# First attention and first feed-forward: pieces placed by a table of times in rounds, and a written order of steps inside a round

## The chip, the cores and the metric

The kernel runs on one core of a Trainium2 chip. The core has a matrix engine (TensorE, PE in the profile), a vector engine (VectorE, DVE), a scalar engine (ScalarE, ACT), GpSimd (POOL), and SyncE (SP), which issues most transfers. Each takes its instructions in the order in which they stand in its queue, and waits by semaphores for the others. The metric is the time of one execution on the device in microseconds, as the median of several runs. Smaller is better.

## The reference

The network has four pairs of attention and feed-forward over x of 2 × 1024 rows and 256 columns. The change touches the first pair, the start of the second attention, and nothing of what they compute:

```python
x = x + _L0_attn_a_ref(_layernorm(x), Wq, Wk, Wv, Wo)
x = x + _L0_ffn_ref(_layernorm(x), W1, b1, W2, b2, W3, b3)
x = x + _L0_attn_b_ref(_layernorm(x), ...)
...
def _L0_attn_a_ref(X, Wq, Wk, Wv, Wo):       # NH, NKV, HD = 16, 8, 32
    q, k, v = heads(X @ Wq), heads(X @ Wk), heads(X @ Wv)
    q = q * cos + _rotate_half(q) * sin
    k = k * cos + _rotate_half(k) * sin
    k, v = repeat(k, 2), repeat(v, 2)
    att = 50 * tanh((q @ k.T) * 256 ** -0.5 / 50)
    att = softmax(where(causal, att, -inf))
    return (att @ v) @ Wo

def _L0_ffn_ref(x, W1, b1, W2, b2, W3, b3):  # 256, 512, 512, 256
    x = relu(x @ W1.T + b1)
    x = relu(x @ W2.T + b2)
    return x @ W3.T + b3
```

`heads` and `repeat` stand here for reshapes and repeats that are written out in the reference.

## The kernel before

`attn_a_ffn0` (line 385) computes the first attention and, between its steps, the feed-forward of rows whose attention is done. All of x stays on the chip as 16 tiles of 128 rows. The two sequences are cut into two chunks of 512 query rows each, so there are four chunks (b, c), numbered 0 to 3 here. A chunk's attention is made of **rounds**: one round takes four heads, one pair of them after another (u and r run over 2 × 2), and one block kb of 128 keys. The first chunk of a sequence sees 4 key blocks, the second 8, so the four chunks have 16, 32, 16 and 32 rounds, 96 in all. Blocks on the diagonal have 512, 384, 256 and 128 live query columns, the others 512.

The steps of a round (`round_`, line 597):

- *scores* (line 611): four matmuls side by side on PE into two PSUM tiles `s` (two buffers, so a round's scores write the tiles that the tanh of the round before has read), then on ACT a tanh (617) for each half into the tile `pr` (four buffers) and an exponential (622) for each half; on diagonal blocks POOL masks each half (625).
- *weigh* (636): four matmuls that add v times `pr` into the one PSUM bank `py`; then on DVE the sums of probabilities are added to `acc` (646, 650, 653). The first block's `pr` is read only by the sums of the second block. After the last block DVE turns `py` (656).
- *finish* (663): the sums are added over partitions by a matmul (`sm`), DVE turns them (668), takes the reciprocal (670), multiplies (671) and turns back into `yT` (674).

Around the rounds stand **pieces**, each a closure that issues instructions on several engines:

- *norms*: for two row tiles, `stats` (251, 252 on DVE, 254 on POOL) and `rows` (the reciprocal root in nine small DVE instructions, 232 to 242, then 263 on POOL);
- *inputs*, nine for each pair of row tiles: `turn` (four transposes, 278, and the copy `xT`, 281, on DVE), `queries` and `keys` (projections `pq` and `pkv`, 290; the rotary part on DVE, 317 and 326, and POOL, 331), `turn_queries` and `turn_keys` (577 and 585 on PE, 578 and 586 on DVE);
- *outputs*, four for each chunk: the projection with Wo (591) and the addition to x (596);
- the 22 pieces of a feed-forward over 512 rows (`ffn0_pieces`, line 461): six for the norms and turns (484 on PE, the copy 492 on DVE, 476 on POOL for b3), four first hidden blocks, four second hidden blocks in two halves each (502 on PE, the relu 511 on DVE), four outputs (518 on PE, 523 on DVE).

The pieces share three PSUM banks (tag `g`). Inside `in_order` the scheduler leaves the order of PE, DVE, ACT and POOL as it is written, so the program text decides the order on every engine. Before the change a planner spreads the pieces: each has a cost (0.35 to 1.75), every round a weight (its columns + 100), `share` gives each round pieces until its share of cost is spent, and `mixed` merges two lists evenly. A round then issues, in this order: scores of round n (with tanh, exponentials and masks), one piece, weigh of round n − 2 (with the sums, and the turn of `py` after the last block), finish of round n − 3 if it was a last block, and the other pieces. The inputs of chunk 0 and the norms of chunk 1 are issued before round 0. Nine pieces of the third feed-forward (`held`) are kept back and merged with the outputs of chunk 3 after the last round. The feed-forward of chunk 3 is done at the start of `attn_b` (line 729), evenly merged (`interleave(owed, chunks[0].inputs)`) with the first inputs of the second attention.

Of the kernel before, what the change touches and what calls it, by code (L numbers as in the profile page):

```python
# [10 lines left out]
F32 = mybir.dt.float32  # L11
I32 = mybir.dt.int32
BF16 = mybir.dt.bfloat16
AF = mybir.ActivationFunctionType
ALU = mybir.AluOpType
# [24 lines left out]
def interleave_into(out, a, b):  # L40
# [56 lines left out]
SECOND = {  # L97
    "norms": (-30, -20.1, -11.8, -12, -6.4, -2.4),
    "unpack": (-7.9, 2.57, (6.7, 7.6, 10.3, 13.8)),
}  # L100


class Net:
# [281 lines left out]
    def attn_a_ffn0(self, w, wo, cos, sin, ffn):  # L385

        nc, tc = self.nc, self.tc
        with ExitStack() as ctx:
            big = ctx.enter_context(tc.tile_pool(name="a_big", bufs=1))
            work = ctx.enter_context(tc.tile_pool(name="a_work", bufs=2))
            ps = ctx.enter_context(tc.tile_pool(name="a_ps", bufs=1, space=PSUM))
            ones = big.tile([P, 32], F32, name="ones")
            nc.gpsimd.memset(ones, 1.0)
            ctx.enter_context(self.in_order())
            pools = (ps, big, work, w, wo, cos, sin, ones)
            chunks = []  # L400
            for b in range(B):


                kT, v = {}, {}
                chunks += [self.attn_a_chunk(pools, b, c, kT, v) for c in range(2)]

            def bank(name):
                return ps.tile([P, 512], F32, tag="g", name=name, bufs=3)


            after = [self.ffn0_pieces(work, bank, 4 * n, *ffn) for n in range(3)]
            for _, step in chunks[0].norms + chunks[0].inputs + chunks[1].norms:
                step()

            def mixed(a, b):
                out = []
                interleave_into(out, a, b)
                return out

            held = 9  # L420
            rounds, fill = [], []
            for chunk, first, second, third in (
                (chunks[0], chunks[1].inputs + chunks[2].norms, [], []),
                (
                    chunks[1], chunks[2].inputs + chunks[3].norms,
                    chunks[0].outputs + after[0], [],
                ),
                (chunks[2], chunks[3].inputs, chunks[1].outputs + after[1][:6], []),
                (chunks[3], after[1][6:], chunks[2].outputs + after[2][:6], after[2][6:-held]),
            ):  # L430

                weights = [r.columns + 100 for r in chunk.rounds]
                quota = sum(weights[:3]) / sum(weights) * sum(
                    cost for cost, _ in first + second + third
                )
                n = 0
                while n < len(first) and quota > 0:
                    quota -= first[n][0]
                    n += 1
                fill += self.share(weights[:3], first[:n])  # L440
                fill += self.share(weights[3:], mixed(first[n:], second) + third)
                rounds += chunk.rounds
            for n in range(len(rounds) + 3):
                here, turned, ended = (
                    rounds[n - j] if 0 <= n - j < len(rounds) else None for j in (0, 2, 3)
                )
                pieces = fill[n] if n < len(fill) else []
                if here:
                    here.scores()
                for piece in pieces[:1]:  # L450
                    piece()
                if turned:
                    turned.weigh()
                if ended and ended.last:
                    ended.finish()
                for piece in pieces[1:]:
                    piece()
            for _, step in mixed(after[2][-held:], chunks[3].outputs):
                step()

    def ffn0_pieces(self, work, bank, i, w1, w2, w3, b1, b2, b3, scalar=False):
# [77 lines left out]
    def attn_a_chunk(self, pools, b, c, kT, v):  # L539
# [58 lines left out]
        def round_(u, r, kb):  # L598
# [5 lines left out]
            def scores():  # L604
                pr = own.pr = work.tile([P, 4, 512], F32, tag="pr", name="pr", bufs=4)
                tiles = [
                    ps.tile([P, 2, 512], F32, tag="s", name="s", bufs=2) for _ in range(2)
                ]
                for s in range(4):
                    rows = slice(32 * s, 32 * s + 32)  # L610
                    nc.tensor.matmul(  # L611
                        tiles[s // 2][:, s % 2, 0:m], kT[kb // 4][rows, u, kb % 4 * P : (kb % 4 + 1) * P],
                        shared["qT"][rows, u, r, off:512], start=True, stop=True,
                    )
                halves = [pr[:, 2 * h : 2 * h + 2, off:512] for h in range(2)]
                for h in range(2):
                    nc.scalar.activation(  # L617
                        halves[h], tiles[h][:, :, 0:m], AF.Tanh, scale=1.0 / (16.0 * 50.0)
                    )
                for h in range(2):  # L620

                    nc.scalar.activation(halves[h], halves[h], AF.Exp, scale=50.0)  # L622
                    if kb >= 4 * c:
                        d = halves[h][:, :, 0:P]
                        nc.gpsimd.affine_select(  # L625
                            out=d, in_=d, compare_op=ALU.is_ge, fill=0.0, base=0,
                            pattern=[[0, 2], [1, P]], channel_multiplier=-1,
                        )

            def weigh():  # L630
                if kb == 0:
# [3 lines left out]
                for s in range(4):  # L635
# [2 lines left out]
                        pr[:, s, off:512], start=(kb == 0), stop=(kb == end),  # L638
                    )

                if kb == 1:
                    acc = shared["acc"] = work.tile(
                        [P, 4, 512], F32, tag="acc", name="acc", bufs=1
# [7 lines left out]
                elif kb > 1:  # L651
                    acc = shared["acc"][:, :, off:512]
                    nc.vector.tensor_tensor(acc, acc, pr[:, :, off:512], ALU.add)
                if kb == end:
                    own.turned = work.tile([P, 16, 32], F32, tag="tny", name="turned", bufs=1)
                    nc.vector.transpose(own.turned.rearrange("p n d -> p (n d)"), py)

            def finish():

# [2 lines left out]
                for s in range(4):  # L662
                    nc.tensor.matmul(
                        sm[32 * s : 32 * s + 32, :], ones, shared["acc"][:, s, :],
                        start=True, stop=True,
                    )
                sums = work.tile([P, 16, 32], F32, tag="tns", name="turned", bufs=1)
                nc.vector.transpose(sums.rearrange("p n d -> p (n d)"), sm)
                rec = work.tile([P, 16], F32, tag="rec", name="rec")
                nc.vector.reciprocal(rec, sums[:, :, 0])  # L670
                nc.vector.tensor_tensor(
# [3 lines left out]
                    shared["yT"][:, 2 * u + r, :], own.turned.rearrange("p n d -> p (n d)")  # L675
                )

            own.scores, own.weigh, own.finish = scores, weigh, finish
            return own

        chunk = type("chunk", (), {})()
# [47 lines left out]
    def attn_b(self, w, wo, cos, sin, ffn):  # L729
# [9 lines left out]
        with ExitStack() as ctx:  # L739
# [25 lines left out]
                return ps.tile([P, 512], F32, tag="sc", name=name, bufs=7)  # L765

            owed = [step for _, step in self.ffn0_pieces(work, bank, 12, *ffn)]
            interleave(owed, chunks[0].inputs)
            quads, rounds, turns, fill = [], [], {}, {}

            def add(n, step):
# [1387 lines left out]
```

## Time and profile before

| | |
|---|---|
| median of 3 runs | 2913.81 us (2906.41, 2915.19, 2913.81) |
| the profiled execution | 2906.75 us |
| its span, first to last instruction | 2905.0 us |
| mean granted TensorE clock | 0.927 |
| busy over the span: PE, weight loads, DVE, ACT, POOL | 87%, 54%, 69%, 46%, 35% |
| first scores (line 611), round 0 | 46.2 us |
| first scores of rounds 16, 48, 64 | 109.9, 238.8, 306.6 us |
| last addition of the stage (line 523) | 453.3 us |
| first scores of the second attention (line 861) | 508.5 us |

The stage that the change touches thus takes about a sixth of the span, from 0 to 508.5 us. A line of the timeline gives the start, the duration, the engine, the line of the kernel, the operation, the output and its inputs, the shapes, how many such instructions are merged, and in brackets how long the engine had been idle and whose result ended the wait. Matmuls overlap and their ends are modelled, so the distance from one start to the next says more than the duration. A matmul on f32 runs as two passes, and appears as two records.

### The profile page before, as it was taken

Reading aid. Unit: us, or ns where it says so; the run is one execution under the profiler, and the core shown is the slowest. Engines: PE = TensorE matmul, PEld = TensorE weight load, DVE = VectorE, ACT = ScalarE, POOL = GpSimd, SP = SyncE. Lnnn points to the kernel's source line nnn. Section 1 sums busy time; section 2 is a strip of 40 time slices with the busy share of each in tenths; the row PEclk is TensorE's granted clock in tenths of the full one; section 3 lists DMA queues with packets and bytes.
Section 4 is the critical chain, followed back from the end, with each engine's and each line's share of the span. In section 5 each row is a group of like instructions: output and inputs, shape, how many; then the busy total and the mean of one; then the engine's idle time right before and its main releaser. Section 6 shows DMA issues by size and latency. Waiting matters only on the chain.

```text
span 2905.0 us, 66838 instructions
## 1 busy us (share of the span) xinstructions
PE 2530.3 (87%) x26384; PEld 1572.5 (54%) x26384; DVE 2003.4 (69%) x6786; ACT 1329.8 (46%) x2800; POOL 1021.7 (35%) x1568
## 2 busy tenths in 40 slices
PE   6999998999998877988888888888787988898888
PEld 2334334444434444665555555555565776777777
DVE  5777774866758957778777878787657555665551
ACT  2676870345453335666666666757321211221110
POOL 3444242211106757667555655655300000000000
PEclk9999998999999967999999999999887998999999
DMA  3000000000001100000000000000011010110100
GB/s 121 1 1 1 1 1 0 1 1 1 1 1 53 36 1 1 1 1 1 1 1 1 1 1 1 1 1 1 20 31 25 10 25 21 21 31 18 24 9 15
DMA packets 61978, 35.37 MB, mean 12 GB/s; under 512 B 43216, under 2 KB 58080, under 8 KB 61664
## 3 DMA queue, kind: packets, MB, share of 16 engines
q1 hardware_dynamic: 59472, 29.49, 3.9%
q8 instruction: 207, 3.39, 0.5%
q10 hardware_dynamic: 2192, 1.61, 0.2%
q14 instruction: 107, 0.88, 0.1%
HBM read 22.68 MB, written 8.39 MB: 11 GB/s over the span
## 4 chain that ended last, share of the span: by engine, by line
PE 39%; DVE 13%; ACT 4%; POOL 4%; issue 4%; DMA 0%; POOLq 0%; ACTq 0%; DVEq 0%
PE ph L1484 5%; PE po L1993 5%; PE pg L1980 5%; PE pu L1980 4%; DVE p L1247 4%; PE e L1236 4%; PE dT L1308 3%; PE po L1503 2%; DVE p L1286 2%; PE py L1338 1%; POOL p L1294 1%; ACT p L1257 1%; POOL p L1274 1%; PE pq L1663 1%; PE kh L1663 1%
## 5 line engine op out<-in xcount | busy, mean ns | idle before, releaser
L1257 ACT ACTIVATE p<-p,nm 128x128 f32<-128x128 f32 (+7 forms) x512 | 390.8, 767 | 78.7 <-DVE nm L1253 40.9
L1247 DVE CUSTOM_DVE_ANT_0 p<-e,mask 128x512 f32<-128x512 f32 (+3 forms) x768 | 382.1, 551 | 59.5 <-PE e L1236 59.1
L1294 POOL TENSOR_SCALAR p<-p,md 128x128 f32<-128x128 f32 (+7 forms) x256 | 241.0, 945 | 175.5 <-DVE md L1286 147.4
L254 POOL TENSOR_SCALAR ln_mv<-ln_mv 128x2 f32<-128x2 f32 x64 | 15.7, 246 | 722.5 <-DVE ln_mv L252 709.6
L1322 ACT ACTIVATE pT<-dT 128x384 f32<-128x384 f32 (+3 forms) x384 | 176.2, 486 | 202.1 <-PE dT L1308 201.2
L1236 PE MATMUL e<-kT,qT 32*128 32x512 f32 (+3 forms) x1536 | 229.8, 578 | 44.3 <-DVE nm L1247 41.5
L1308 PE MATMUL dT<-ident,p 128*128 128x128 f32 x1152 | 197.0, 297 | 65.8 <-POOL p L1294 35.6
L1286 DVE CUSTOM_DVE_ANT_0 p<-p,nrs 128x128 f32<-128x128 f32 (+7 forms) x256 | 220.3, 885 | 24.7 <-POOL p L1278 24.4
L901 ACT ACTIVATE pr<-s 128x512 f32<-128x512 f32 (+3 forms) x384 | 157.3, 497 | 162.9 <-PE s L896 154.2
L1274 POOL TENSOR_SCALAR p<-p,ra,neg_lam 128x128 f32<-128x128 f32 (+7 forms) x256 | 217.8, 851 | 9.3
L1308 PEld LDWEIGHTS dT<-ident,p 128*128 128x128 f32 x1152 | 137.6, 149 | 153.1 <-POOL p L1294 67.7
L617 ACT ACTIVATE pr<-s 128x1024 f32<-128x1024 f32 (+1 forms) x192 | 145.3, 813 | 131.0 <-PE s L611 83.5
L1993 PE MATMUL po<-down,inter 128*128 128x256 f32 x576 | 160.1, 441 | 1.9 <-DVE x L2000 1.2
L861 PE MATMUL s<-kT,qT 32*128 32x512 f32 (+3 forms) x768 | 155.3, 519 | 3.8 <-DVE q_pad L869 1.9
L1980 PE MATMUL pg<-xT,gate 128*128 128x256 f32 x576 | 151.1, 409 | 5.5 <-ACT xT L283 5.5
L622 ACT ACTIVATE pr<-pr 128x1024 f32<-128x1024 f32 (+1 forms) x192 | 152.1, 852 | 0.0
L869 DVE CUSTOM_DVE_ANT_0 masked<-s,mask 128x128 f32<-128x128 f32 (+3 forms) x256 | 110.6, 487 | 58.9 <-PE s L861 58.8
L1236 PEld LDWEIGHTS e<-kT,qT 32*128 32x128 f32 x1536 | 84.8, 202 | 116.4 <-DVE nm L1247 74.3
L625 POOL TENSOR_SCALAR_AFFINE_SELECT pr<-pr 128x256 f32<-128x256 f32 x128 | 90.1, 722 | 154.7 <-ACT pr L622 57.7
L1986 DVE TENSOR_TENSOR inter<-inter,pu 128x512 f32<-128x512 f32 x72 | 49.3, 684 | 132.7 <-PE pu L1980 132.7
L1993 PEld LDWEIGHTS po<-down,inter 128*128 128x128 f32 x576 | 126.4, 224 | 25.0 <-DVE x L2000 2.0
L1980 PE MATMUL pu<-xT,up 128*128 128x256 f32 x576 | 139.3, 386 | 0.0
(295 smaller groups left out, 5377.2 us busy)
## 6 DMA issues: line engine op xcount, KB each, us to landing
uk_d<-uk SPq DMA_DIRECT2D x128, 32.0 KB, 1.9
r<-uk_d SPq DMA_DIRECT2D x8, 512.0 KB, 3.6
x<-in_L_attn_a_X SPq DMA_DIRECT2D x4, 512.0 KB, 6.9
qh_d<-qh SPq DMA_DIRECT2D x8, 256.0 KB, 2.6
o<-qh_d SPq DMA_DIRECT2D x128, 16.0 KB, 1.7
out<-x SPq DMA_DIRECT2D x4, 512.0 KB, 3.1
w<-in_L_ffn_W2T SPq DMA_DIRECT2D x1, 1024.0 KB, 7.5
pk<-in_L_ffn_gate_packed SPq DMA_DIRECT2D x8, 128.0 KB, 2.5
```

The source lines that it names most:

```text
L861: nc.tensor.matmul(tiles[g][:, 0:n], shared["qT"][rows, t, j * P : (j + 1) * P], kT[rows, lo : lo + n], start=True, stop=True,)
L901: nc.scalar.activation(pr[:, g, off:512], tiles[g][:, 0:m], AF.Exp, scale=0.25)
L1236: nc.tensor.matmul(own.tiles[h][:, a, 0 : hi - lo], made["q"][r : r + 32, a, t, :], kT[r : r + 32, a, lo:hi], start=True, stop=True,)
L1247: nc.vector.tensor_tensor_reduce(own.p[h][a][:, lo:hi], own.tiles[h][:, a, 0 : hi - lo], neg_row[:, T - nk + lo : T - nk + hi], -1.0, 3e38 ...
L1257: nc.scalar.activation(own.p[h][a], own.p[h][a], AF.Exp, bias=own.nm[:, h, a : a + 1], scale=-1.0, accum_out=own.sm[:, h, a : a + 1],)
L1274: nc.gpsimd.tensor_scalar(p1, p1, own.ra[:, h : h + 1], nlam[:, head : head + 1], ALU.mult, ALU.mult)
L1286: nc.vector.tensor_tensor_reduce(p0, p0, p1, own.nrs[:, h : h + 1], 3e38, ALU.add, ALU.min, own.md[:, h : h + 1],)
L1294: nc.gpsimd.tensor_scalar(p0, p0, -1.0, own.md[:, h : h + 1], ALU.mult, ALU.add)
L1308: nc.tensor.transpose(dT[:, n, :], own.p[h][0][:, kb * P : (kb + 1) * P], self.ident)
L1322: nc.scalar.activation(shared[t, s + h][:, lo:hi, :], own.dT[h, part][:, 0 : hi - lo, :], AF.Exp)
L1980: nc.tensor.matmul(ph[:, j, :], m_[:, kc, m * P : (m + 1) * P], f.xT[:, kc, :], start=(kc == 0), stop=(kc == 1),)
L1993: nc.tensor.matmul(f.po[:, b], inter[m // 2][:, m % 2, b * P : (b + 1) * P], wd[:, m % 2, (m // 2) * C : (m // 2 + 1) * C], start=(m == 0) ...
```

## The change

A table `FIRST` gives each piece a time, counted in rounds: negative before round 0, 42.12 for shortly after the start of round 42. All pieces of the stage are put in one list and sorted by it. The steps of a round are split into smaller ones (`scores`, `tanh` and `exp` for each half, `weigh`, `sums`, `turn`, `finish`, `divide`), and the string `round` writes their order: scores, sums, tanh 0, tanh 1, exp 1, exp 0, finish, divide, weigh, turn. `lags` says how many rounds later a step is done. A piece is issued ahead of the step at whose tenth of the round its time falls. Pieces whose times lie behind the last round are issued afterwards. The hand-over to the second attention gets two lists of times of its own.

```diff
+FIRST = {
+    "lags": {"W": 2, "Z": 2, "V": 2, "F": 3, "G": 3},
+    "round": "S Z A0 A1 B1 B0 F G W V",
+    "inputs": (
...
+        (
+            12.2, 13.35, 14.1, 15.15, 16.37, 17.33, 18.16, 23.08, 24.51, 24.94, 25.12,
+            26.54, 27.81, 28.92, 29.68, 30.61, 31.63, 32.76, 33.49, 34.5, 35.34, 34.505,
+        ),
...
+    "ffn": (
+        (
+            26, 26.35, 26.005, 28.76, 29.61, 34.99, 35.96, 36.52, 37.92, 38.3, 39.37,
+            40.663, 41.655, 41.968, 41.973, 41.978, 42.12, 42.137, 43.63, 44.17, 45.33,
+            46.22,
+        ),
...
+    "owed": (
+        0, 1, 2, 2.8, 4.09, 5.62, 6.071, 6.77, 8.216, 8.915, 9.869, 10.824, 12.589, 12.601,
+        13.614, 14.709, 16.685, 17.762, 18.073, 19.179, 20.299, 21,
+    ),
+    "next": (
+        -1.5, 1.69, 4.79, 4.795, 7.431, 9.276, 13.151, 16.167, 16.172, 17.387, 17.392,
+        18.948, 19.543, 19.834, 23.309, 23.314, 28.039, 29.57,
+    ),
+}
...
-            held = 9
-            rounds, fill = [], []
-            for chunk, first, second, third in (
...
-                fill += self.share(weights[:3], first[:n])
-                fill += self.share(weights[3:], mixed(first[n:], second) + third)
-                rounds += chunk.rounds
-            for n in range(len(rounds) + 3):
...
-            for _, step in mixed(after[2][-held:], chunks[3].outputs):
-                step()
+            timed = []
+            for n, chunk in enumerate(chunks):
+                timed += zip(FIRST["inputs"][n], [s for _, s in chunk.norms + chunk.inputs])
+                timed += zip(FIRST["outputs"][n], [s for _, s in chunk.outputs])
+                if n < 3:
+                    pieces = self.ffn0_pieces(work, bank, 4 * n, *ffn)
+                    timed += zip(FIRST["ffn"][n], [s for _, s in pieces])
+            timed.sort(key=lambda x: x[0])
+            rounds = [r for chunk in chunks for r in chunk.rounds]
+            tokens = FIRST["round"].split()
...
+            for n in range(len(rounds) + 4):
+                for k, token in enumerate(tokens):
+                    while timed and (timed[0][0] - n) * len(tokens) <= k + 1e-6:
+                        timed.pop(0)[1]()
+                    m = n - FIRST["lags"].get(token[0], 0)
+                    if 0 <= m < len(rounds) and hasattr(rounds[m], names[token[0]]):
+                        getattr(rounds[m], names[token[0]])(*[int(x) for x in token[1:]])
+            for _, step in timed:
+                step()
...
-            interleave(owed, chunks[0].inputs)
+            timed = list(zip(FIRST["owed"], owed)) + list(zip(FIRST["next"], chunks[0].inputs))
+            for _, step in sorted(timed, key=lambda x: x[0]):
+                step()
```

By these times the PE pieces stand like this in some rounds (h is a first hidden block, h2 half of a second one, between two scores in program order): round 23 a query projection and an output; 41 to 42, after the scores of 41, one h2, weigh, three h2, the scores of 42, two h2, sums matmul, weigh; 49 three projections; 69 three outputs; 64, 88, 91 and 94 none. Chunk 0's inputs take the two query projections of a pair of tiles ahead of its key projections. The third feed-forward keeps its last nine pieces, and chunk 3 three of its four outputs, until after the last round, the outputs first.

## The prediction

> **What bounds the kernel now.** I looked first at the busy time by stretches, cut where the four chunks of the first stage begin: rounds 0–15 start at 46.2 us, rounds 16–47 at 109.9, 48–63 at 238.8, 64–95 at 306.6; the last chunk's end runs from 423.7, and the hand-over to the second attention ends at 508.5. After the span come PE, weight loads, DVE, ACT and POOL busy, then the granted clock.
>
> ```profile
> core 0: us, PE busy (x) PEld busy (x) DVE busy (x) ACT busy (x) POOL busy (x), PEclk, DMA share, GB/s
> 46.20:109.90 63.70, 53.77 (x329) 19.52 (x328) 45.23 (x109) 39.96 (x64) 28.53 (x53) 0.89 0.01 1
> 109.90:238.80 128.90, 123.94 (x732) 46.55 (x728) 98.61 (x167) 100.59 (x128) 53.85 (x59) 0.99 0.00 1
> 238.80:306.60 67.80, 60.01 (x397) 25.51 (x393) 51.48 (x105) 40.99 (x67) 36.01 (x59) 0.95 0.00 1
> 306.60:423.70 117.10, 115.78 (x676) 42.81 (x676) 81.94 (x100) 99.11 (x124) 36.30 (x40) 1.00 0.00 1
> 453.70:508.50 54.80, 41.19 (x136) 22.96 (x136) 26.50 (x84) 3.40 (x8) 17.11 (x35) 0.84 0.00 0
> ```
>
> TensorE (PE) is the bound in every row. The long chunks have little left (PE busy 96% and 99%); both short chunks lose on idle time and on the clock. What a loss looks like, in the timeline at round 16:
>
> ```profile
> 109.94 1.14 PE L611 MATMUL s<-qT,kT 32*128 32x512 f32 x8
> 111.02 0.66 PE L278 MATMUL ln_t<-ident,ln_xn 128*128 128x128 f32 x4
> 111.60 0.64 PE L636 MATMUL py<-pr,v 128*32 128x256 f32 x8
> 114.81 1.98 PE L290 MATMUL pq<-wa,xT 128*128 128x512 f32 x4 [2.58 <-DVE xT L281]
> ```
>
> PE turns the normalised rows at 111.02, and wants the copy (xT, line 281) for its next projection. That copy stands on DVE behind another chunk's norm and the row sums, so PE idles 2.58 us.
>
> **Prices of a round.** I take start to next start, since ends are modelled:
>
> ```profile
> 415.23 1.06 PE L636 MATMUL py<-pr,v 128*32 128x512 f32 x8
> 416.23 1.08 PE L611 MATMUL s<-qT,kT 32*128 32x384 f32 x8
> 417.24 1.99 PE L502 MATMUL ph<-h,w 128*128 128x512 f32 x4
> 419.15 1.07 PE L636 MATMUL py<-pr,v 128*32 128x512 f32 x8
> ...
> 155.46 1.94 ACT L617 ACTIVATE pr<-s 128x1024 f32<-128x1024 f32 x2 [1.47 <-PE s L611]
> 157.28 2.00 ACT L622 ACTIVATE pr<-pr 128x1024 f32<-128x1024 f32 x2
> 159.17 1.02 ACT L617 ACTIVATE pr<-s 128x1024 f32<-128x1024 f32 x1
> ```
>
> Weigh 1.00; one piece (projection or hidden half) 1.91; scores of 512 columns 1.07 (109.94 to 111.02). ACT needs 159.17 − 155.46 = 3.71 for a round of 512 columns; the same view gives 2.86, 2.00 and 1.16 for 384, 256 and 128. So a full round has 3.71 − 2.07 = 1.64 us of PE time beside ACT, somewhat less than one piece. For each round I add the PE steps standing between two scores, in program order, and take the larger of that and ACT. Done over 95 rounds of the old order, most rounds agree with the trace within 0.1 us; what is measured above the sum is stalls and slow clock.
>
> | rounds | PE steps before | larger, before | measured | remainder | larger, after |
> |---|---|---|---|---|---|
> | 0–15 | 45.1 | 48.0 | 63.75 | 15.8 | 51.5 |
> | 16–47 | 119.0 | 121.7 | 128.9 | 7.2 | 127.0 |
> | 48–63 | 55.7 | 57.3 | 67.75 | 10.5 | 58.4 |
> | 64–94 | 110.7 | 116.5 | 117.1 | 0.6 | 118.2 |
>
> **The change, part by part.** No instruction of the stage is added or taken; the compiled order shows other places on PE, DVE and POOL, and ACT's two exponentials swapped. DMAs and SP's queue keep their places, so nothing is moved past a transfer.
>
> *The table* lumps pieces. Round 42 gets five hidden halves (three ahead of its scores), while rounds 64, 65, 88 and 91 get no piece for PE between their scores, or none but small ones. Hence the sums after: +3.5, +5.3, +1.1, +1.7, together 11.6 us worse. ACT's backlog over such a row gives back a little: rounds 80 to 82 measure 11.71 where the larger values add to 12.35. I take 0.5 in each long chunk, −1.0.
>
> *The remainders* are what it can win.
> - Rounds 48–63: the largest stall is 2.76 us at 240.5–242.9, xT again. In the new table the turn is in round 48 and its projection in 49, the norm four rounds earlier; key and query turns come a round or more after their ropes. I leave 2.0 of 10.5: −8.5.
> - Rounds 0–15: rounds 0 and 1 lose 7.6 between them (scores wait for ACT and xT). The new order puts scores 1 ahead of the first turn, so ACT has work during the projection; DVE's second norm still comes first. I leave 5.6 there. DVE's own work in rounds 12–15 sums to 14.7 us in the new order and 14.4 in the old, so 2.0 of the rest stays: 7.6 of 15.8, −8.2.
> - Rounds 16–47: the 2.58 us above goes, as its turn is now a round ahead. DVE's sum in rounds 24–31 is 30.4, a microsecond above PE and ACT. I leave 1.5 of 7.2: −5.7.
> - Rounds 64–94: −0.6.
>
> *Sums (Z) ahead of pieces on DVE.* ACT waits 38 us in all for a probability buffer until the sums have read it; Z at the front ends that. This is inside the remainders. Z waits for POOL's masks two rounds old; behind it stand the pieces' evacuations, and PE's three small banks cover a round.
>
> *Ends.* The first chunk's inputs now run q0, q1 ahead of k0, and DVE's xT ahead of the second norm (xT was 1.16 us late): scores 0 come 1.2 earlier after a wait for the last key turn. At the end two hidden halves fill the wait for the masks at 424–429 us, which lengthens S95-to-sums by 0.7 while the rounds above lose 2.6 of PE work, counted there. All four outputs now follow the division directly: the first needs yT, DVE's four steps after the sums (0.72+0.26+0.69+0.71 = 2.4 less 1.2 of its own early matmuls), +1.2, where a hidden half stood before. In the hand-over the second half's norm comes one norm (1.6 us) earlier on DVE; a later turn costs 0.6: −1.0.
>
> *Clock.* Thin rounds may slow PE. Rows:
>
> ```profile
> 239.40:242.80 3.40, 1.19 (x12) 0.42 (x4) 3.29 (x3) 2.39 (x4) 3.40 (x3) 1.00 0.00 0
> 242.80:246.20 3.40, 3.06 (x10) 1.22 (x11) 1.50 (x2) 1.47 (x2) 3.06 (x6) 0.51 0.00 0
> ...
> 147.20:150.60 3.40, 2.72 (x20) 0.89 (x18) 3.33 (x8) 3.40 (x5) 1.06 (x1) 1.00 0.00 0
> 150.60:154.00 3.40, 3.31 (x4) 1.17 (x4) 3.06 (x15) 3.39 (x4) 1.54 (x3) 0.51 0.00 0
> ```
>
> A stretch with sparse matmuls is followed by 3.4 us at 0.51, which costs PE 1.7. Bounds: none (rounds 72 and 73, PE 3.5 and 3.3 of 3.71, stayed at 1.00) or one after each of nine runs of thin rounds, 15. Rounds 25, 64 and 88 have PE for 1.6 to 1.8 of 3.71, nearest to the second pair; for those three I take 3 in all.
>
> The Trainium skill ("TensorE: Matmul & The Clock Gate", HAM oscillation) gives as its rule no PE gap over about 3.4 us. By that rule the thin rounds, idle at most 2.1 us at a stretch (3.71 − 1.64), would cost 0 in place of 3; the rows above, where gaps of 1 to 2.8 us were enough, speak against relying on it.
>
> Sum: +11.6 − 1.0 − 8.5 − 8.2 − 5.7 − 0.6 − 1.2 + 0.7 + 1.2 − 1.0 + 3.0 = −9.7; the bounds of the two large unknowns are remainders wholly gone but for rounds 0–1 (−5.5 more), or kept (+23), and clock 0 to 15 (−3, +12). The profiled execution took 2906.75 us (span 2905.0); −9.7 gives 2897.1. The median of the three runs is 2913.81, 7.1 higher, which gives 2904.1. I predict between them: **2900 us**.
>
> **Rivals.**
> 1. *Stalls all go, and so does the slow clock.* Remainders to 5.6, clock term 0: −18; the hand-over, where PE idles 13.6 of 54.8 us, gives 5 more: about −23, 2887. For: the new distances between producer and consumer. Against: DVE's 14.7 in rounds 12–15 stays. 0.20.
> 2. *No change to tell.* The remainders keep some 20 of their 34, as DVE, not the order on PE, sets them: the lumps' 11.6 meets 14 won, and the ends and clock add 2: 2910 ± 5. For: POOL's masks stretch beside DVE's sums in any order (line 625 takes 0.41 us at best, 0.71 in the mean). Against: in chunk 3 the same sums leave 0.6. 0.20.
> 3. *Slower: the clock.* Each of the nine runs of thin rounds lets the clock fall for two stretches of 3.4 us: 18 × 1.7 = 31 in place of 3, 2928. It decides from about nine stretches on (9 × 1.7 − 3 = 12). For: 147.2 needed only a part-idle stretch. Against: half of the runs fill PE for 60% of ACT's time. 0.12.
> 4. *That the tables don't bite* is excluded: the compiled order moves on three engines.
>
> The forecast itself has 0.48: 2890 to 2908.
>
> **How the numbers follow.** 0.3%, about what a measurement here can tell from no change, is 8.7 us, 2905 to 2922.5 around the median. The forecast puts 0.40 of its 0.48 under 2905, rival 1 all 0.20: faster 0.60. Rival 2 has 0.15 within, 0.05 above; the forecast's other 0.08 falls within: same 0.23. Rival 3's 0.12 and that 0.05: slower 0.17. The range takes in rival 1's middle and most of the lower half of 3: 2878 to 2922.
>
> **What would show it.** Right: scores 16, 48 and 64 begin near 104, 232 and 293 us; the wait for xT at line 281 gone from the short chunks; rounds 41 and 42 with PE full and ACT idle for some 8 us; rounds 64 and 88 paced by ACT. Wrong: DVE sums still among ACT's waits, or a granted clock below 0.95 in rounds 64 to 95. If rounds 48–63 don't fall below 64 us, the main term has failed.

## The result, and the profile after

The changed kernel takes 2887.84 us in the median of five runs (2884.38 to 2897.69), the kernel before 2906.41 us beside it (2901.01 to 2915.19). The ratio is 0.9935, with a 95% interval from 0.9907 to 0.9964. The profiled execution took 2885.65 us, its span is 2883.9 us, the mean granted clock 0.931. Repeated later on one chip with other kernels, it gave 2889.29 us and 0.9925 (0.9908 to 0.9943). So the change is worth some 19 to 22 us, about twice the 9.7 us that the prediction's sum gave.

The busy time by stretches, cut again at the first scores of rounds 0, 16, 48, 64 and 95, with the hand-over last (after the span come PE, weight loads, DVE, ACT and POOL busy, then the granted clock):

```profile
40.80:96.60 55.80, 51.01 (x329) 19.50 (x328) 45.17 (x108) 41.08 (x62) 31.13 (x52) 0.91 0.01 1
96.60:226.80 130.20, 125.95 (x736) 48.11 (x732) 102.56 (x169) 104.32 (x130) 53.38 (x62) 0.97 0.00 1
226.80:285.40 58.60, 56.36 (x388) 23.97 (x385) 47.30 (x94) 42.75 (x66) 31.28 (x53) 1.00 0.00 1
285.40:403.20 117.80, 114.33 (x676) 42.80 (x676) 83.74 (x108) 100.92 (x122) 35.75 (x43) 1.00 0.00 1
434.50:489.20 54.70, 40.86 (x132) 23.19 (x132) 27.99 (x85) 2.41 (x6) 17.41 (x35) 0.84 0.00 0
```

The rows say where. Rounds 48 to 63 fall from 67.8 to 58.6 us and their clock rises from 0.95 to 1.00. Rounds 0 to 15 fall from 63.7 to 55.8 us and begin 5.4 us earlier. The long chunks (second and fourth row) take what they took. From the first scores to those of round 95 PE idles for 14.5 us instead of 23.6 (gaps of more than 0.15 us between its matmul records), and the clock is at half for 17.1 us instead of 23.9, which is worth up to 3.4. These two make 12.5 of the 15.1 us that the kernel wins there.

| part | forecast | measured, profiled executions |
|---|---|---|
| head, to the first scores | −1.2 | −5.4 (46.19 to 40.77; −4.4 in the repeat, 41.84) |
| rounds 0–15 | −4.7 | −7.9 |
| rounds 16–47 | −0.9 | +1.2 (−0.5 in the repeat) |
| rounds 48–63 | −7.4 | −9.1 |
| rounds 64–94 | +0.6 | +0.7 |
| scores of round 95 to the stage's last addition | +1.9 | +1.6 |
| hand-over | −1.0 | −0.4 |
| clock, as a term of its own | +3.0 | none; it is in the rows above |
| rest of the program, unchanged | 0 | −1.8 |
| sum | −9.7 | −21.1 |

What ACT waits for ahead of its tanh (one group before, one after: busy time and mean, then idle time and its releasers):

```profile
L617 ACT ACTIVATE pr<-s 128x1024 f32<-128x1024 f32 (+3 forms) x190 | 144.7, 817 | 129.9 <-PE s L611 82.3 <-DVE acc L646 27.8 <-DVE acc L653 10.1
```
```profile
L652 ACT ACTIVATE pr<-s 128x1024 f32<-128x1024 f32 (+1 forms) x192 | 144.3, 803 | 99.1 <-PE s L644 92.9 <-DVE acc L685 5.9
```

Of the 37.9 us in which DVE's sums held ACT up, 5.9 are left. The largest such place is round 16, in the timeline of the changed kernel:

```profile
97.11 0.71 DVE L717 STREAM_TRANSPOSE yT<-turned 128x512 f32<-128x512 f32 x1
97.74 1.72 DVE L685 TENSOR_TENSOR acc<-pr 128x1536 f32<-128x1536 f32 x1
99.55 1.94 ACT L652 ACTIVATE pr<-s 128x1024 f32<-128x1024 f32 x2 [2.17 <-DVE acc L685]
100.63 2.99 PE L644 MATMUL s<-qT,kT 32*128 32x512 f32 x8 [1.67 <-ACT pr L652]
102.50 0.69 DVE L340 TENSOR_SCALAR xT<-ln_t 128x512 f32<-128x512 f32 x1
```

Here the division of a finished block (its last step is the turn into `yT`) is on DVE ahead of the sums, the sums hold ACT, ACT holds PE's scores, and a norm's root then stands between the sums and the copy xT. The stall of round 16 that the prediction showed has changed its first link and has not gone.

### The profile page after: what moved, and what is told of

Same layout as the page of the kernel before. It is cut to its first block, busy times and chain, and to the rows that moved or that the text cites. A ratio compares the mean times of both kernels' runs of the same rounds, so it can differ in the third digit from the quotient of the medians.

```text
span 2883.9 us, 66846 instructions
## 1 busy us (share of the span) xinstructions
PE 2519.9 (87%) x26384; PEld 1569.8 (54%) x26384; DVE 2005.4 (70%) x6786; ACT 1340.7 (46%) x2800; POOL 1020.5 (35%) x1568
## 4 chain that ended last, share of the span: by engine, by line
PE 39%; DVE 14%; ACT 4%; POOL 4%; issue 3%; DMA 0%; POOLq 0%; DVEq 0%; SPq 0%; ACTq 0%
PE ph L1531 6%; PE po L2040 5%; PE pg L2027 5%; PE pu L2027 4%; DVE p L1294 4%; PE e L1283 4%; PE dT L1355 3%; PE po L1550 2%; DVE p L1333 2%; PE py L1385 1%; POOL p L1341 1%; ACT p L1304 1%; PE pq L1710 1%; POOL p L1321 1%; PE kh L1710 1%
```

## The experiments

All times to a point of the program are of one profiled execution; ratios are medians against the kernel before on the same chip. "Slow clock" is the time before the scores of round 95 in which the granted clock was about half (the clock records; each stretch is a multiple of 3.41 us). The records begin with the first stretch at full clock, at 22.3 us in the changed kernel and 27.8 us before; ahead of it the matmuls of a projection start 0.85 us apart, behind it 0.43, and this slow start isn't in the column.

| kernel | median | ratio, 95% interval | first scores | from there to round 95 | from there to attn_b's first scores | slow clock |
|---|---|---|---|---|---|---|
| before | – | 1 | 46.19 | 377.5 | 84.8 | 27.3 |
| changed | 2887.84 | 0.9935 (0.9907–0.9964) | 40.77 | 362.5 | 86.0 | 17.1 |
| e0 changed again | 2889.29 | 0.9925 (0.9908–0.9943) | 41.84 | 361.2 | 86.0 | 13.7 |
| e1 old head order | 2893.58 | 0.9945 (0.9925–0.9964) | 44.30 | 363.6 | 85.8 | 23.9 |
| e2 xT late | 2909.22 | 0.9993 (0.9978–1.0007) | 41.16 | 379.3 | 86.0 | 37.6 |
| e3 sums late | 2903.30 | 0.9978 (0.9964–0.9993) | 42.70 | 377.0 | 86.2 | 34.1 |
| e4 filled | 2894.67 | 0.9941 (0.9918–0.9963) | 41.82 | 373.2 | 76.6 | 30.7 |
| e5 before, sums first | 2905.90 | 0.9982 (0.9969–0.9995) | 43.89 | 370.9 | 82.5 | 17.1 |
| e6 before, head and xT | 2901.35 | 0.9965 (0.9951–0.9978) | 41.31 | 371.9 | 86.1 | 20.5 |
| e7 before, all three | 2892.36 | 0.9933 (0.9913–0.9952) | 42.65 | 368.5 | 82.3 | 20.5 |
| e8 filled, mended | 2876.58 | 0.9885 (0.9869–0.9901) | 42.03 | 360.5 | 77.2 | 13.7 |
| e9 filled, mended again | 2877.97 | 0.9886 (0.9867–0.9906) | 41.95 | 362.0 | 77.4 | 23.9 |
| e10 bare rounds | 2895.37 | 0.9941 (0.9920–0.9962) | 42.31 | 363.0 | 86.5 | 17.1 |

### e1: the head in its old order

```diff
 "inputs": ( (
-  -48, -46.195, -45.41, -43.685, -44.19, -43.2, -42, -42.995, -42.695, -38.4, ...
+  -48, -47, -46, -44, -45, -43, -42, -41, -40, -39, ...
```

> The changed kernel with one part of its table undone: chunk 0's projections stand in their old order (q and k of the two halves mixed, each followed by its rotated twin), instead of both q first; xT of the first half still stands ahead of the second norm, and everything from round 0 on is as in the changed kernel. Theory (the order of the projections gave most of the 5.4 us by which round 0 came earlier: 46.19 to 40.77 in the two profiled executions): the scores of round 0 start at 45 to 46.5 again, and the end comes 4 to 5.5 us later than the changed kernel's 2883.9, at 2888 to 2889.5. Rival (only the place of xT counts, which the prediction priced at 1.2 us, and the rest was where the slow-clock stretches happened to fall): the scores of round 0 start at 40 to 43 and the end is within 2 us of 2883.9. What tells them apart is the start of the first scores and the granted clock between 20 and 45 us.

The first scores start at 44.30 us, between what theory (45 to 46.5) and rival (40 to 43) named: 3.5 later than the changed kernel's, and attn_b's first scores come 4.5 later. The medians (0.9945 and 0.9935) can't tell the two kernels apart. PE in the head, first before, then e1, then the changed kernel:

```profile
18.35 3.78 PE L290 MATMUL pq<-wa,xT 128*128 128x512 f32 x4 [1.93 <-DVE xT L281]
23.22 3.75 PE L290 MATMUL pkv<-wa,xT 128*128 128x512 f32 x4 [1.08 <-DMA wa<-in_L_attn_a_Wv]
```
```profile
16.82 3.47 PE L318 MATMUL pq<-wa,xT 128*128 128x512 f32 x4 [0.78 <-DVE xT L309]
23.78 3.39 PE L318 MATMUL pkv<-wa,xT 128*128 128x512 f32 x4 [3.48 <-DMA wa<-in_L_attn_a_Wv]
```
```profile
16.77 6.42 PE L349 MATMUL pq<-wa,xT 128*128 128x512 f32 x8 [0.83 <-DVE rsq_n L291]
23.04 0.38 PE L610 MATMUL t_ps<-ident,qr 128*128 128x128 f32 x2
23.66 0.44 PE L610 MATMUL t_ps<-ident,qr 128*128 128x128 f32 x2 [0.24 <-POOL qr L390]
23.93 3.61 PE L349 MATMUL pkv<-wa,xT 128*128 128x512 f32 x8
```

In before and e1 the key projection waits for a transfer, the weights from Wv. With xT early and the old order PE starts its first query projection at 16.82 instead of before's 18.35, and then idles 3.48 us instead of 1.08 at that wait. The new order puts the second query projection, which needs only weights that are there, into the wait: in the changed kernel Wv's transfer is issued at 16.7 us and lands 6.6 us later, and no wait on it is listed.

Of e1's 3.5 us, some 2.0 are the order and 1.4 the clock. From the key projection to the first scores e1 takes 20.52 us, the kernel before 22.97, and e5 (below, which has before's head) 19.08. The differences are about half of the time at half clock: e1 has such a stretch at 23.3 to 26.7 us, at the end of the idle time; before reaches full clock only at 27.8 us and has a slow stretch at 34.6; e5 is at full clock from 23.2 us on. The ten executions with the new order take 23.8 to 24.0 us from the first query projection to the first scores, with no slow stretch in it. e5 takes 24.62 and begins 1.1 us later, for xT. So xT and the order together are worth some 1.7 us, and the rest of what before loses in the head is mainly the clock.

### e2: xT directly ahead of its reader

```diff
 chunk 1, second turn    -6.35   +8.398     (query projection at 8.4)
 chunk 2, both turns     -16.37  +17.328    -28.92  +29.678
 chunk 3, both turns     -48.01  +49.248    -56.55  +57.853
```

> The changed kernel with the five transposing copies (xT) of chunk 1's second half and of chunks 2 and 3 set directly ahead of the first projection that reads them, as the old planner set them, instead of about one round ahead; every other step keeps its time. Theory (the distance between the copy and its reader is what took the stalls out of rounds 0 to 63): each of the five costs a wait of 1 to 2.8 us on PE again, the waits on xT are back in the list, rounds 48 to 63 go from 58.7 to 61 to 64 us and the whole is 5 to 13 us longer than the changed kernel's 2883.9. Rival (the stalls went because the softmax sums now stand first on DVE, so that the copy itself is done sooner): the waits on xT stay under 0.5 us each, and the whole is within 2 us.

The stage takes 17.2 us more (attn_b's first scores 489.21 to 506.43), above the 5 to 13 expected; rounds 48 to 63 take 64.2 us, at the upper edge. PE's waits by releaser, e2 and the changed kernel from 36 to 430 us (total, times, longest):

```profile
PE pq L318 <- DVE xT L309: 10.9, 6, 4.3
PE s L613 <- ACT pr L621: 10.2, 13, 2.2
```
```profile
PE s L644 <- ACT pr L652: 9.3, 11, 1.7
PE pq L349 <- DVE xT L340: 1.6, 2, 1.0
```

The waits on xT grow by 9.3 us, and all of PE's listed waits together by 6.4 (16.7 to 23.1, since others fall away). The slow clock grows by 20.5 us, which at half speed is worth up to 10.2. Together 16.6, against 17.2 measured: the larger part of these stalls' price is the clock behind them. The rival (under 2 us) is out. The old planner had some of the five turns farther ahead than e2 has, so e2 prices the distance; it doesn't undo the change.

### e3: the sums behind the weighing

```diff
-  "Z": "sums", "V": "turn",
+  "Z": "none", "V": "late",
...
+def late():
+    sums()
+    if kb == end:
+        turn()
```

> The changed kernel with the step Z (the softmax sums on DVE, which free the tanh's output buffers for ACT) put back behind the weighing step, with the V step as before the change; the times of all pieces are kept. Theory (that Z stands ahead is what took the 27.8 and 10.1 us of DVE out of ACT's waits ahead of the tanh): 15 to 40 us of ACT's idle time ahead of the tanh end on DVE's sums again, and because ACT paces the rounds without pieces, the attention stage grows by 3 to 6 us. Rival (ACT was waiting for PE's scores all along and the name of the releaser is all that changes): the time is within 1.5 us of the changed kernel's 2883.9 though DVE is back among the releasers.

```profile
L621 ACT ACTIVATE pr<-s 128x1024 f32<-128x1024 f32 (+1 forms) x192 | 144.2, 802 | 114.4 <-PE s L613 83.9 <-DVE acc L654 25.5 <-POOL pr L630 2.7
```

In this group of e3, DVE's sums hold ACT for 25.5 us again, as the theory said, but the stage takes 16.6 us more (505.83) instead of 3 to 6. PE's listed waits grow by 5.6 us (16.7 to 22.3): on ACT's tanh 13.7 (9.3 in the changed kernel), 3.4 on `acc` ahead of the sums' matmul, while others are shorter. The slow clock grows by 17 us, half of which is 8.5. Together 14.1, against 14.7 counted from the first scores (1.9 of the 16.6 were there already). The rival falls.

### e5, e6, e7: the parts alone on the old grid

e5 takes the kernel before and only moves the sums ahead; e6 only takes the new head order and the turns of rounds 16 and 48 one round earlier; e7 has both.

```diff
 if here:
     here.scores()
+if turned:
+    turned.sums()          # e5, e7; taken out of weigh
 for piece in pieces[:1]:
...
+for n in (16, 48):         # e6, e7
+    fill[n - 1].insert(0, fill[n].pop(0))
...
-for _, step in chunks[0].norms + chunks[0].inputs + chunks[1].norms:
+for k in (0, 1, 2, 4, 3, 5, 7, 8, 6, 9, 10, 12, 13, 11, 14, 16, 15, ...):
```

> The kernel before with one part of the change alone: the softmax sums of a round stand directly behind the scores on DVE (ahead of the round's pieces and of the weighing), the planner, its grid of pieces and the head stay as they were. The previous runs gave 16.6 us (to the first scores of attn_b) for putting the sums back, far over the forecast. Theory (the parts add up, each stall on PE bringing a slow-clock stretch behind it): 10 to 16 us shorter than before's 2905.0, ACT's idle time on DVE's sums falls from 37.9 us to under 10, and the slow-clock time before the last scores falls from 27.3 us to about 17. Rival (the order of the sums pays only together with the new times of the pieces, because in the old grid other things are late at the same places): within 4 us of 2905.0 although ACT no longer waits for DVE.

> The kernel before with two other parts alone: the head's pieces in the new order (chunk 0's two q projections one behind the other, xT ahead of the second norm), and the xT of chunks 2 and 3 that the old grid had in the same round as its first reader (rounds 16 and 48) one round earlier. Sums, grid and hand-over stay. Theory: the head gives its 4 to 5.5 us by itself (first scores at 40.7 to 42), and the two moved copies 2 to 5 us more in rounds 16 to 63 (the waits on xT there, up to 2.6 us each, gone, and a slow-clock stretch less): 2895 to 2899. Rival (what the head gains is lost again in round 1, which waits for the next norm): rounds 0 to 15 grow by what the head gave, and the end is within 2 us of 2905.0.

> The kernel before with all three small parts (sums ahead, the head's new order, xT of rounds 16 and 48 a round earlier), but with the old planner's grid of pieces and the old hand-over. It differs from the changed kernel by the grid alone. Theory (the prediction's sum: the new times of the pieces pair them worse with the rounds and cost 11.6 us in lumps, which the stalls' end had to pay for): this kernel is faster than the changed one by 5 to 12 us, at 2872 to 2879. Rival (the grid's spacing is itself what keeps DVE and POOL from being late, and the sum over rounds overstates the lumps): slower than the changed kernel by 2 to 10 us, at 2886 to 2894, with waits on POOL's masks and turned copies left.

e5: attn_b's first scores come at 497.3 instead of 508.5, −11.1, with ACT's waits on the sums at 12.4 us (not quite under 10) and 17.1 us of slow clock. Of the 11.1 us, 2.3 lie ahead of the first scores, where e5 changes nothing. The median shows half of the 11.1 (ratio 0.9982, about −5). e6: −9.1 in the stage and 0.9965, about −10; the first scores come at 41.31, as its theory had it, and rounds 0 to 15 give back 1.1 (64.8 us). e7: −14.9 in the stage and 0.9933, which is −19.5 in the median. The parts add up only roughly (−20 for e5 and e6 in the stage, −15 in the medians), but the three together reach the time of the changed kernel (0.9935 and 0.9925).

So no worth of the grid of pieces and the hand-over, beyond the three parts, shows in the medians, and e7's theory, that the grid costs 5 to 12 us, falls. Its rival holds in the time (2892.36, named 2886 to 2894), and in part in the releasers: turned copies are there, but waits on POOL's masks are 0.9 us, and the norms, which it didn't name, are the most. e7's waits of PE, from 38 to 424 us:

```profile
PE ln_t L492 <- POOL ln_xn L263: 6.0, 3, 2.7
PE pq L290 <- DVE xT L281: 4.8, 3, 2.3
PE s L619 <- ACT pr L625: 3.5, 3, 1.9
PE ln_t L278 <- POOL ln_xn L263: 3.0, 1, 3.0
```

The old grid turns rows whose norm POOL has not finished (9.0 us), and reads xT too early three times (4.8). The table has none of the first and 1.6 of the second. By the prediction's sum of the larger of PE and ACT, the old grid has 343.6 us up to round 95 and the new one 355.2. e7 takes 368.5, that is 25 above its sum; the changed kernel 362.5, that is 7.3 above. By this reckoning the lumps cost what the prediction said, 11.6, and the spacing between producer and reader wins 17.7; no run has the one without the other. Behind round 95 e7 is 3.7 us shorter (82.3 to 86.0).

### e4, e8, e9: thin rounds filled

In e4 the rounds in which PE had less than ACT get pieces that stood later, so that five pieces (9.5 us) fewer are left behind the last scores. e8 and e9 move norms that were then late. The main lines of the edits (e8 also moves two of the `xT` turns by some 0.4 of a round, and two turns of the feed-forward):

```diff
 inputs of chunk 2 (e4; an output of chunk 3 goes from 99 to 99.5)
-  16.37, 17.33, 18.16, 23.08, 24.51, 24.94, 25.12, ...
+  15.3,  16.37, 17.33, 18.1,  19.2,  20.2,  21.2, ...
 feed-forward of chunks 1 and 2 (e4)
-  65.15, 65.13, 66.1, 67.9, 68.787, 71.873, ...   84.69, 86.876, 89.572, 92.127, ...
+  62.1,  62.85, 64.15, 65.3, 66.2,  68.3, ...      83.3,  84.2,  85.2,  86.1, ...
 norm pieces of the feed-forwards (e8)
-  24, 24.35, 26.005, ... 27.61     60.08, 61.67, ... 62.85
+  23.6, 24.35, 24.7, ... 25.6      59.2, 59.9, ... 60.7
 second norms of chunks 1 and 2 (e8)
-  -18, -16.06      14.1, 15.15
+  3.3, 5.05        17.8, 19.3
 norm pieces (e9)
-  59.2, 59.9, 62.1, 60.7, 64.5
+  60.08, 61.3, 62.1, 63.05, 64.95
```

> The changed kernel with other times in its table: the rounds of chunks 1 and 3 in which PE had less than ACT (25, 30, 64, 88 to 91 and their like) get pieces of the feed-forward and of the next chunk's projections that stood later, so that five half-rounds of pieces fewer are left behind the last softmax round; the last output piece of the stage stands half a round later, with a feed-forward piece ahead of it to fill its wait. Theory (the stage is paced by the larger of PE and ACT in each round, as the prediction's sum has it): the sum up to the last scores is 355.6 us, as the changed kernel's 355.2, and 9.5 us less is left behind them; with some stalls coming back the end moves by -4 to -9 us, to 2875 to 2880. Rival (PE is bound by its whole work in any order, and the sum over rounds measures nothing): within 1.5 us of 2883.9.

> The filled table of the previous run (e4_filled) with its two new stalls taken away: the feed-forward's second normalisation stands ahead of the key rotation on POOL instead of between them, and in rounds 59 to 64 two rounds ahead of the transposes that read it; besides, the second half's normalisations of chunks 1 and 2 stand later, behind the xT copy that rounds 1 and 16 wait for. Theory (what e4_filled lost were these two waits, 3.3 and 3.8 us, and the slow clock behind them, 8 us): the first scores of attn_b come at 477 to 482 instead of 491.6 and the whole is 2872 to 2877. Rival (the lost time comes from pieces filling the rounds as such): within 3 us of e4_filled, first scores of attn_b at 489 to 494.

> e8_filled2 with its one remaining long stall taken away: in rounds 60 and 61 POOL's normalisation for the feed-forward stood ahead of the key rotation and of the masks (PE waited 3.5 us for a mask, and a slow-clock stretch followed); the normalisation goes one round later for the first half and three for the second, behind the key rotations. Theory: rounds 48 to 63 fall from 61.9 to 58 to 59.5 us, and the first scores of attn_b come at 475 to 478 instead of 479.7; the median is 2870 to 2875. Rival (another engine's queue is then late at the same place, as it was in e4_filled): rounds 48 to 63 stay at 61 to 63 us.

e4 gained its 9.4 us behind round 95 (76.6 instead of 86.0) and lost 10.7 ahead of it, so that both its theory and its rival missed (2892.0 us in the profile). PE's waits in two places of e4, one that ends near 165 us and one near 297 us:

```profile
PE t_ps L587 <- POOL kr L359: 3.3, 1, 3.3
```
```profile
PE ln_t L486 <- POOL ln_xn L291: 3.8, 1, 3.8
```

In both, a norm of the feed-forward had come to stand on POOL a round too close: ahead of a key rotation, or ahead of the turn that reads it. With those moved, e8 keeps the 8.8 us behind round 95 and takes 360.5 us ahead of it, where the sum of the larger, as worked out for e4, is 355.6. Its 2876.58 us and 0.9885 lie below both kernels, and its interval (0.9869 to 0.9901) below both intervals of the changed kernel. The theory of e8 is right in the stage (479.70, forecast 477 to 482).

e8 has one long stall left, PE waiting 3.5 us for a mask behind POOL's norm and rotation in round 61. e9 took it away and won 1.2 of the 2.4 to 3.9 us in rounds 48 to 63 (60.74), because another norm was then late in round 64, and rounds 64 to 94 lost 2.6:

```profile
PE ln_t L486 <- POOL ln_xn L291: 2.5, 1, 2.5
```

The 60.74 lies between what theory and rival named, but what happened is the rival's picture, and the median (0.9886) is the same as e8's.

### e0 and e10: spread, and the clock in thin rounds

> The changed kernel once more, for the spread of a profiled execution (first scores and what follows the stage), beside e9 and e10 on one chip. Theory (over the runs so far the new head gave first scores at 40.8 to 42.7, the old one at 43.9 to 46.2, so the changed kernel's 40.8 was at the early end): first scores at 41 to 43, first scores of attn_b at 489 to 492, 2884 to 2890 in the median. Rival (40.8 is what this kernel does): first scores within 0.3 us of 40.8.

e0 is the changed kernel unchanged. Its first scores at 41.84 and attn_b's at 489.06 bear the theory out: 40.77 was an early draw, and round 0 starts at 40.8 to 42.7 us in the ten executions with the new head and at 43.9 to 46.2 in the three with the old order of projections.

```diff
 feed-forward of chunk 2 (e10)
-  84.69, 86.876, 89.572, 92.127, 93.684, 95.639
+  84.69, 86.876, 92.05, 93.05, 94.05, 95.639
```

> The changed kernel with three pieces of the feed-forward moved out of rounds 89 to 93 into 92 to 94, so that rounds 87 to 91 have no piece at all: PE has 1.2 to 3.0 us of work in rounds that ACT makes 3.7 long. The larger-of sum grows by 1.5 us. Theory (in the runs so far each 3.41 us clock stretch in which PE was busy for less than half was followed by a stretch at half clock, 17 of 17): one or two slow stretches appear between 385 and 400 us, where the changed kernel has none, and rounds 64 to 94 take 1.5 to 4 us more than its 117.8. Rival (rounds paced by ACT don't bring the slow clock, only true stalls do, so that the prediction's 3 us for thin rounds were wrong in kind): no slow stretch there, and rounds 64 to 94 take 119 to 119.5 us.

Two stretches of the clock in the changed kernel (rounds 63 to 65), in which PE is busy for 2.28 and 2.10 of 3.40 us and no slow one follows, and three in e10 (rounds 88 to 91):

```profile
281.70:285.10 3.40, 2.28 (x24) 0.63 (x24) 3.30 (x7) 2.64 (x7) 2.70 (x8) 1.00 0.02 5
285.10:288.50 3.40, 2.10 (x18) 0.80 (x20) 3.40 (x4) 1.53 (x3) 2.10 (x2) 1.00 0.00 0
```
```profile
380.50:383.90 3.40, 2.83 (x24) 0.76 (x16) 1.94 (x3) 3.37 (x4) 1.62 (x2) 1.00 0.00 0
383.90:387.30 3.40, 1.99 (x11) 0.62 (x11) 0.72 (x1) 3.37 (x5) 0.00 (x0) 1.00 0.00 0
387.30:390.70 3.40, 3.40 (x18) 0.59 (x16) 1.35 (x3) 3.37 (x4) 0.00 (x0) 0.50 0.00 0
```

In e10 the bare rounds bring one slow stretch, at 387.3 us, after one in which PE was busy for 1.99 of 3.40. So rounds paced by ACT can slow the clock, as the theory said, in this one execution. But rounds 64 to 94 take 119.73 us, 1.9 more than the changed kernel's 117.8, of which 1.5 are the larger sum: the slow stretch itself cost some 0.4. ACT, which paced those rounds, is busy for 3.37 of 3.40 us in it. The rival is wrong about the cause and nearly right about the time.

## Why the prediction was right, and where not

The direction, the mechanism and the place are right: the change wins by stalls ended in rounds 0 to 15 and 48 to 63. Rounds 48 to 63, which it named as its test at 64 us, take 58.7. Its size is short by half: 2887.84 us lies outside the 2890 to 2908 of the forecast itself and on rival 1's 2887, and inside the stated 2878 to 2922 because that takes the rival in. Some 3 us of the distance to 2900 are the base, as the kernel before ran at 2906.41 beside it. By its own steps:

- **Head, −1.2.** Mis-sized: −5.4, or −4.4 in the repeat. xT's place gave what the step said (PE waits 0.83 us ahead of the first projection instead of 1.93). The step left out the wait for Wv at 23.22 us and the clock. Against e5, which has the same head, xT and the order win 1.7 us; of the other 3.7 some 3 are the slow clock of before's one execution (27.84 us from the first projection to the first scores, e5 24.62), and the rest is an earlier start. So over half of the 5.4 is a draw, though in the ten executions of the new order no slow stretch falls there.
- **Rounds 0–15, 7.6 left of 15.8.** 4.3 are left. Rounds 0 and 1 lose 3.5 between them, where the step left 5.6: round 1 takes 8.34 us and loses 5.0, at xT (1.0) and in a stretch at half clock, and round 0, at 2.25, is 1.5 under ACT's 3.71. The 2.0 left for DVE's load in rounds 12 to 15 was too much.
- **Rounds 48–63, 2.0 left of 10.5.** 0.2 are left, but the step read its largest stall wrongly, and that the number fits is in part luck. The trace of before lists no wait on xT in these rounds. The 2.55 us up to 243.14 ended with a mask of POOL, which had been at a norm since 237.99:

```profile
237.99 4.73 POOL L263 TENSOR_SCALAR ln_xn<-x,ln_mv,rsq_y 128x256 f32<-128x256 f32 x2 [1.57 <-DVE rsq_y L242]
243.14 1.43 PE L636 MATMUL py<-pr,v 128*32 128x256 f32 x8 [2.55 <-POOL pr L625]
```

PE's other long waits there were 2.4 us on the turn of `py` and 1.9 on ACT. In the changed kernel 0.6 on masks, 0.7 on ACT and 0.9 on a query copy are left, and the 6.8 us at half clock are gone. The norm four rounds earlier, which the step also named, fits this. e2 shows that a late xT can bring such a loss back (64.2 us, with 1.6 of waits on xT and 10.2 at half clock); it doesn't show that xT was the cause before.
- **Rounds 16–47, 1.5 left of 7.2.** 3.1 are left (1.4 in the repeat): the stall of round 16 that was to go came back by the sums behind a block's division, as the timeline above shows.
- **Sums ahead, "inside the remainders".** Right, and a large part: behind the first scores, e5 and e3 give 9 and 15 us to that step (8.8 won, 14.7 lost), though in the medians e5 wins 5 and e6, head and xT, about 10. ACT's waits on DVE fell from 37.9 to 5.9, not to none; sums among ACT's waits were a sign of being wrong by the prediction's own list.
- **Lumps, +11.6.** Argued, not shown: sum and measurement of the changed kernel agree within 7.3 us over 95 rounds, but no run takes the lumps away alone. e8 shows that thin rounds can take more PE work (five pieces pulled ahead of round 95). The prediction set the lumps against the stalls of the old order; by the same sum e7 has 17.7 us more of these than the table.
- **Clock, +3.0.** Wrong in sign. Rounds 64 to 95 stayed at 1.00, and the slow clock of the stage fell from 27.3 to 17.1 us (13.7 in the repeat), worth up to 5 to 7 us (1.7 of them are the head's, above). The step asked where thin rounds would slow PE; the stalls taken away were what had slowed it. The remainders had this price in them, since they were measured with the clock, but it wasn't traced to each stall. The gaps in the rows that the step shows are 0.8 and 2.55 us, a little less than the 1 to 2.8 that it names.
- **Ends, +1.9 and −1.0.** +1.6 and −0.4.
- **What would show it.** Scores 16, 48 and 64 start 5 to 8 us earlier than named (96.6, 226.8, 285.4), by the head and the first chunk. Rounds 41 and 42 have PE full (8.69 and 6.56 us) and ACT idle 7.0. ACT's pace shows one round behind the thin ones: rounds 64 and 65 take 2.69 and 3.85, rounds 88 and 89 2.25 and 4.24.

Rival 1, at 2887, has the time but not all of its picture: waits of 17 us in all and 17.1 us of slow clock remain in the stage, and the hand-over gave 0.4 of its 5. Its sum is met because the head and the distances gave more. Rivals 2 and 3 are out.

What stays open: how much each part is worth alone. The median of e5 shows half of what its profiled stage shows; the profiled execution (2898.87 us) is the fastest of its ten, whose median is 2905.90, and 2.3 us of its gain are the draw of the head. The unchanged rest of the program took 2391.2 to 2404.1 us over these thirteen executions, a spread larger than most of the differences in question, so single executions can't settle it.

## What to carry to other kernels

A stall of the matrix engine is priced as its idle time and the half-speed stretch that may follow it; a stall that ends takes both away. When a written order replaces a planner, look first at each producer's distance in its own queue (norm, rotation, mask and copy on DVE and POOL) and only then at how evenly the bound engine is loaded: even filling (e4) was lost mainly to two norms a round too close, and paid in full once they were moved (e8). In a head, order the work by when its weights land.

## What the runs showed of the hardware

The clock changes only on a fixed beat. Within a trace every change lies a multiple of 3.413 us from every other. Cut on that beat, and taking those that lie wholly between 40 and 425 us in all thirteen profiles, the stretches at full clock were followed by one at half clock as follows (PE busy as the union of the matmul records, as a share of the stretch):

| PE busy in the stretch | stretches | followed by half clock |
|---|---|---|
| under 0.5 | 18 | 18 |
| 0.5 to 0.8 | 110 | 31 |
| over 0.8 | 1237 | 0 |

This can account for the same order drawing other slow stretches from one execution to the next. A stall of 2 us slows the clock when it falls within one beat: nine of the 18 have a single gap of 1.9 to 2.4 us. It may not when a beat divides it: the 2.58 us stall of before at round 16, from 112.2 to 114.8 us, has a beat in it at 113.1, left PE busy for 0.51 of the stretch behind that, and no slow stretch followed. The Trainium skill ("TensorE: Matmul & The Clock Gate", What's actually happening) says the activity window is about 3.4 us long and runs freely, not started by the kernel; the traces agree (a beat of 3.413 us, whose place against the first instruction differs by up to 2.6 us between the executions). Its rule for real kernels (HAM oscillation), that PE gaps be kept to some 3.4 us or less, falls short here: in the stretch ahead of e10's slow one the longest wait listed for PE was 1.46 us, and half a beat of idle time was always enough, in three of the 18 stretches in two pieces, none of them over 2.1 us.

The rest of the program, the same instructions in every kernel, varied by 12.9 us between executions, and with it its time at half clock: 356.1 us in e8 (2391.2 from attn_b's first scores to the end), 393.7 in e3 (2404.1).
